# Normalisation parameters and biases of images 1 to 7 computed through device memory and VectorE in a two-layer convolution block

## The chip, the cores and the metric

The kernel runs on one core of a Trainium2 chip. The metric is the device time of one execution in microseconds (us), the median of three runs. The engines are TensorE (PE in the profile; PEld is its weight load), VectorE (DVE), ScalarE (ACT), GpSimd (POOL) and SyncE (SP). Each works through its own list of instructions in order and waits on semaphores for the others. DMAs are issued from SP, ACT or POOL.

## What is computed

Eight images of 384 channels and 64 x 64 positions go through two residual blocks, each with a group normalisation ahead of it (32 groups of 12 channels). Layer 0 is linear attention with rotary positions, layer 1 a gated convolution with an 8 x 8 FFT filter. Cut to what the change touches:

```python
def _gn(v, G=32, eps=1e-5):
    g = v.reshape(B_, G, C_ // G, H_, W_)
    m = jnp.mean(g, axis=(2, 3, 4), keepdims=True)
    s = jnp.var(g, axis=(2, 3, 4), keepdims=True)
    return ((g - m) / jnp.sqrt(s + eps)).reshape(v.shape)

q = apply_rope_2d(conv1x1(x, Wq, bq))
k = apply_rope_2d(conv1x1(x, Wk, bk))
v = conv1x1(x, Wv, bv)
q = jax.nn.elu(to_heads(q) * scale) + 1.0
k = jax.nn.elu(to_heads(k)) + 1.0
kv = jnp.einsum('bhnd,bhne->bhde', k, v)
out = jnp.einsum('bhnd,bhde->bhne', q, kv) / (normalizer + 1e-06)
...
x = x + _L0_conv_ref(_gn(x), ...)
x = x + _L1_conv_ref(_gn(x), ...)
```

## The kernel before

Channels lie on the 128 partitions in three tiles (CT = 3), positions in eight bands of 512. All data are f32. The kernel walks over the images; within one image there are two stages.

*Query stage* (`queries`). For each band, `q_project` (L598) multiplies x with the query weights; DVE adds the bias and turns by the rotary tables (L610, L627), ACT and DVE make elu plus one (L337 to L339); `q_normalise` (L636) and `q_spread` (L660) bring in the normaliser, whose reciprocal DVE writes as `parts` (L652); `project_out` (L677) multiplies with the folded matrix `mt`. At the head of the stage the sums over keys of this image are finished: `kx` is copied by ACT (L566), POOL spreads the key sums into `ks_bd` (L498), DVE puts the heads with the value bias into `kvt_bd` (L571), PE transposes it (`pt`, L583), ACT copies it (`kvt`, L584), PE multiplies (`pm`, L508) and ACT copies `mt` (L515).

*Layer-1 loop.* For each band, layer 1 of this image runs: input projection `pi` (L695), DFT, filter, inverse DFT, the depthwise taps on DVE (L798, `dw`), the gate and the output projection `pw`. Filled in between are the key and value projections (`pk` L438, `pv` L454) and the key sums of the next image. The last band's taps and output run in the next query stage; two of its taps are added by POOL's DMA (`tap`, L781).

Layer 0's normalisation is folded into the weights: the inverse deviation of each channel's group scales the rows of `wk`, `wq` and `wv` (`scale_weight`, L352), and what the mean takes off becomes a bias. The statistics of the next image are streamed during the layer-1 loop (`stream_stats`); what is left is a chain of small steps, `norm_chain`, written as a generator with a `yield` after each step. The query stage of image b pulls it for image b + 1: twice in each of bands 2 to 5, so that its steps lie between the large matmuls. The steps are:

- `mean_and_variance` on DVE (L202 to L207) gives the mean and variance of each channel, `mv`.
- Group mean: three matmuls with a membership matrix (`ps_m`, L273), a copy to `gm` (L291).
- Back to channels: three matmuls (`ps_mc`, L281), difference and square on DVE (L294 to L298).
- Group variance: `ps_v` (L273), `var` (L301), square root on ACT (L303), reciprocal and one Newton step on DVE (L304 to L310).
- Back to channels: `ps_r` (L281), `rs` (L313), and `shift`, minus mean over deviation for each group (L319).

`wk` is then scaled, and `k_bias` (L357, `pbk`) multiplies `shift`, broadcast over 128 columns, with the group sums of the key weights, which `sum_weight` made once with PE (`pg_wk` and others, L345). The result, one row of 384 on all partitions, is added to `bk` (L359). `q_bias` (L365, `pbq`, three matmuls of one column) does the same for the query bias in band 4 of the layer-1 loop, `v_bias` (L375, `pbv`) for the value bias at its end. An f32 matmul counts as two instructions of PE in the profile.

The order of instructions on each engine is not that of the program text: a scheduler places them when the program is built, by priorities and its own estimate of times, and adds all semaphore waits. POOL also issues the DMAs that add layer 1's result to the output in device memory (`out_dram<-y`, L861), and sets the ones columns of the value tiles (`v`, L411). SP issues all other DMAs.

Of the kernel before, what the change touches and what calls it, by code (L numbers as in the profile page):

```python
# [24 lines left out]
NG = 32  # L25
GROUP = C // NG
# [91 lines left out]
def conv_blocks_kernel(ctx: ExitStack, tc: tile.TileContext, a: dict, out: bass.AP, nb: int):  # L118
    nc = tc.nc

    const = ctx.enter_context(tc.tile_pool(name="const", bufs=1))
# [3 lines left out]
    qp = ctx.enter_context(tc.tile_pool(name="qp", bufs=2))  # L125
    small = ctx.enter_context(tc.tile_pool(name="small", bufs=2))
    psum = ctx.enter_context(tc.tile_pool(name="psum", bufs=8, space=bass.MemoryType.PSUM))

    def ps_tile(name):
        return psum.tile([P, 512], F32, tag="ps", name=name)  # L130

    def w_tile(shape, name):
        return work.tile(shape, F32, tag="w", name=name)
# [18 lines left out]
    stats, moments = {}, {}  # L152
# [54 lines left out]
        nc.vector.scalar_tensor_tensor(mv[:, :, 1], s_[:, :, 1], 1.0 / N, s_[:, :, 0], ALU.mult, ALU.subtract)  # L207
        return mv

    group_w = {}  # L210

    for j in range(NBAND - 1):
        load_x(0, j)
# [28 lines left out]
    ident = groups[:, 2 * CT * NG :]  # L242
    of_group = const_tile([NG, C], "of_group", a["of_group"])
    first_wk = load_weight(0, "wk", k_runs)
    load_x(0, NBAND - 1)
    bk_bc = const_tile([P, C], "bk_bc", a["bk"].partition_broadcast(P), nc.sync)
    scale = HD ** -0.5
    halves = (slice(0, 64), slice(64, P))
    w_out = const.tile([P, 2, C], F32, tag="w_out", name="w_out")
# [14 lines left out]
    def norm_chain(b, layer, params):  # L264


        n = f"{layer}_{b}"
        mv = mean_and_variance(b, layer)

        def group_mean(src, name):  # L270
            ps = ps_tile(name)
            for t in range(CT):
                nc.tensor.matmul(  # L273
                    ps[:NG, 0:1], to_group[:, t, :], src[:, t : t + 1], start=(t == 0), stop=(t == CT - 1)
                )
            return ps[:NG, 0:1]

        def to_channels(src, name):
            ps = ps_tile(name)
            for m in range(CT):  # L280
                nc.tensor.matmul(  # L281
                    ps[:, m : m + 1], of_group[:, m * P : (m + 1) * P], src, start=True, stop=True
                )
# [24 lines left out]
        nc.vector.tensor_mul(y, y, var)  # L308
        nc.vector.tensor_scalar(y, y, -0.5, 1.5, ALU.mult, ALU.add)
        nc.vector.tensor_mul(rsg, rsg, y)  # L310
        yield
        rs = small.tile([P, CT], F32, tag=f"rs{layer}", name=f"rs{n}")
        nc.vector.tensor_copy(rs, to_channels(rsg, f"ps_r{n}"))  # L313
        nb_ = small.tile([P, CT], F32, tag=f"nb{layer}", name=f"nb{n}")
        nc.vector.tensor_mul(nb_, minus_mean, rs)  # L315
        params += rs, nb_
        if layer == 0:
            shift = group_tile("shift")
            nc.vector.scalar_tensor_tensor(shift, gm, -1.0, rsg, ALU.mult, ALU.mult)  # L319
            params.append(shift)  # L320

    def normalised(b, j, params, order, name):

        rs, nb_ = params
        h = w_tile([P, CT, BT], f"h{name}_{b}_{j}")
        for t in range(CT):
            dst, src = h[:, t, :], xt[b, j][:, t, :]
            if order is not None:
                blocks, width = order
                dst = dst.rearrange("p (b r c) -> p r b c", b=blocks, r=8, c=width)  # L330
                src = src.rearrange("p (r b c) -> p r b c", b=blocks, r=8, c=width)
            nc.scalar.activation(dst, src, AF.Identity, bias=nb_[:, t : t + 1], scale=rs[:, t : t + 1])  # L332
        return h
# [4 lines left out]
        nc.scalar.activation(e, e, AF.Exp, scale=-1.0)  # L338
        nc.vector.scalar_tensor_tensor(x_, x_, 0.0, e, ALU.max, ALU.add)  # L339

    def sum_weight(w, name):

        p_ = ps_tile(f"pg_{name}")
        for t in range(CT):
            nc.tensor.matmul(p_[:NG, :C], member[:, t, :], w[:, t, :], start=(t == 0), stop=(t == CT - 1))  # L345
        t = const.tile([NG, C], F32, tag=f"group_{name}", name=f"group_{name}")
        nc.scalar.copy(t, p_[:NG, :C])
        group_w[name] = t

    def scale_weight(w, params, factor=1.0):  # L350
        for i in range(CT):
            nc.vector.tensor_scalar(w[:, i, :], w[:, i, :], params[0][:, i : i + 1], factor, ALU.mult, ALU.mult)  # L352

    def k_bias(b, params):

        p_ = ps_tile(f"pbk_{b}")
        nc.tensor.matmul(p_[:, :C], params[2].to_broadcast([NG, P]), group_w["wk"], start=True, stop=True)  # L357
        t = small.tile([P, C], F32, tag="kbias", name=f"kbias_{b}", bufs=1)
        nc.vector.tensor_add(t, p_[:, :C], bk_bc)  # L359
        return t  # L360

    def q_bias(b, params):
        p_ = ps_tile(f"pbq_{b}")
        for m in range(CT):
            nc.tensor.matmul(  # L365
                p_[:, m : m + 1], group_w["wq"][:, m * P : (m + 1) * P], params[2], start=True, stop=True
            )
        t = small.tile([P, CT], F32, tag="qbias", name=f"qbias_{b}")
        nc.vector.scalar_tensor_tensor(t, p_[:, :CT], scale, bqs, ALU.mult, ALU.add)
        return t  # L370

    def v_bias(b, params):

        p_ = ps_tile(f"pbv_{b}")
        nc.tensor.matmul(p_[:, :C], params[2].to_broadcast([NG, P]), group_w["wv"], start=True, stop=True)  # L375
        t = small.tile([P, C], F32, tag="vbias", name=f"vbias_{b}", bufs=1)
        nc.vector.tensor_add(t, p_[:, :C], bv_bc)
        return t

    transposed = {}

# [481 lines left out]
    def layer0_chain(b, prepared):  # L866

        if b >= nb:
            return
        wk = load_weight(b, "wk", k_runs) if b else first_wk  # L870
        params = []
        if b == 0:
            sum_weight(wk, "wk")
        yield from norm_chain(b, 0, params)
        scale_weight(wk, params)
        yield
        prepared += params, wk, k_bias(b, params)

    def chain_of(*chains):
        for c in chains:  # L880
# [8 lines left out]
    class Keys:  # L889


        def __init__(self, b, prepared):
            self.b, self.live = b, b < nb
            if self.live:
                self.params, self.wk, self.bias = prepared
                self.kf = {}

        def project_k(self, j):
# [39 lines left out]
        def prepare(self, j):  # L938

            if self.live and j == 4:  # L940
                self.wq = load_weight(self.b, "wq", QRUNS)
                if self.b == 0:
                    sum_weight(self.wq, "wq")
                scale_weight(self.wq, self.params, scale)
                self.qbias = q_bias(self.b, self.params)
            if self.live and j == NBAND:
                self.wfc = load_weight(self.b, "wfc", k_runs)
                if self.b == 0:
                    self.wv = load_weight(self.b, "wv", k_runs)
                    sum_weight(self.wv, "wv")  # L950
                self.vbias = v_bias(self.b, self.params)

    def queries(b, keys, before_last, late):

# [63 lines left out]
    prepared = []  # L1018
# [1 line left out]
    keys = Keys(0, prepared)  # L1020
    run(keys.project(0))

    bv_bc = const_tile([P, C], "bv_bc", a["bv"].partition_broadcast(P), nc.sync)
    bq = const.tile([P, CT], F32, tag="bq", name="bq")
    for c0, at, n in QRUNS:

        t, p0, quarter, first = at // P, at % P, c0 // QC, c0 % QC
# [15 lines left out]
    for half in halves:  # L1043
        nc.sync.dma_start(w_out[half, 1, :], a["w_out"][P : P + 64, :])

    bqs = const.tile([P, CT], F32, tag="bqs", name="bqs")
    nc.vector.tensor_scalar_mul(bqs, bq, scale)

    filt = const.tile([P, C], F32, tag="filt", name="filt")

# [108 lines left out]
    b = nb - 1  # L1159
# [60 lines left out]
```

## Time and profile before

| | |
|---|---|
| Time, three runs | 3364.33 us median (3363.24 to 3365.47) |
| Span of the profiled execution | 3364.3 us |
| Mean granted TensorE clock | 0.992 |
| Instructions | 53556 |
| HBM read, written | 232.70 MB, 99.88 MB |

A profile shows one execution. Busy time of an engine is the time in which its instructions run; register, branch and semaphore instructions and the issuing of DMAs do not count as busy, apart from what POOL spends on its DMAs' descriptors. The chain of waits goes back from the last instruction to what released each step. In a timeline a row is a run of like instructions: start, duration, engine, line, operation, what it writes and reads, count, and, in brackets, how long the engine stood idle before it and what ended that. PE's matmuls are pipelined, so the duration of a row is longer than its distance to the next one. In the DMA table the last number is the median time from issue to landing.

### The profile page before, as it was taken

To read this page: it belongs to the slowest core of one execution; us is meant where nothing else is said; L and a number is where in the kernel's file an instruction comes from. 1 tells how busy PE (TensorE), PEld (TensorE's weight loads), DVE (VectorE), ACT (ScalarE), POOL (GpSimd) and SP (SyncE) were. 2 spreads that over 40 slices of the span, in tenths; PEclk is the share of its full clock that TensorE was granted. 3 is DMA by queue.
4 is the path that set the end of the run, shared out by engine and by line. 5 is a ranking of instruction groups with operands and counts; after the bars stand their busy time and mean duration, and the time that the engine had idled before them with its cause. 6 is when DMAs were issued, how large, how long until landed. Compare 5 with 4: busy or idle time off the path is not lost.

```text
span 3364.3 us, 53556 instructions
## 1 busy us (share of the span) xinstructions
PE 3300.1 (98%) x21370; PEld 1851.9 (55%) x21370; DVE 2752.5 (82%) x4517; ACT 2034.0 (60%) x4039; POOL 128.8 (4%) x261
## 2 busy tenths in 40 slices
PE   8999999999999999999999999999999999999987
PEld 5544566456654566545665456654566445664454
DVE  6577789967889688896888968888788877989698
ACT  4445666566665566655666656656576565556563
POOL 0000000000000000000000000000000000000000
PEclk9999999999999999999999999999999999999999
DMA  6323335342443423533335343443333431324113
GB/s 217 111 94 100 95 78 128 111 136 67 109 116 110 137 67 94 131 107 120 85 88 126 109 120 76 106 129 107 102 96 94 133 115 54 85 70 121 62 24 53
DMA packets 151502, 343.37 MB, mean 102 GB/s; under 512 B 27365, under 2 KB 38613, under 8 KB 143061
## 3 DMA queue, kind: packets, MB, share of 16 engines
q1 hardware_dynamic: 123844, 282.85, 25.0%
q0 software_dynamic: 27216, 56.89, 11.4%
q8 instruction: 168, 2.75, 0.3%
q14 instruction: 82, 0.66, 0.1%
q10 hardware_dynamic: 192, 0.21, 0.0%
HBM read 232.70 MB, written 99.88 MB: 99 GB/s over the span
## 4 chain that ended last, share of the span: by engine, by line
PE 81%; DVE 11%; ACT 6%; issue 1%; DMA 1%; SPq 0%; DVEq 0%; ACTq 0%
PE pf L677 15%; PE pi L695 14%; PE pk L438 13%; PE pv L454 13%; PE pq L598 9%; DVE dw L798 4%; PE pw L831 4%; PE pb L730 3%; PE pd L709 2%; PE pw L842 2%; PE acc L470 2%; PE acc L483 2%; PE pn L636 1%; ACT qs L338 1%; ACT qs L337 1%
## 5 line engine op out<-in xcount | busy, mean ns | idle before, releaser
L798 DVE SCALAR_TENSOR_TENSOR dw<-ring,w_dw,dw 128x512 f32<-128x512 f32 x1401 | 976.4, 744 | 245.3 <-ACT ring L746 206.2
L438 PE MATMUL pk<-wk,x 128*128 128x384 f32 x1536 | 544.9, 496 | 0.0
L598 PE MATMUL pq<-x,wq 128*128 128x512 f32 x1152 | 527.6, 605 | 2.6 <-ACT mt L515 2.6
L695 PE MATMUL pi<-w_in,hf 128*128 128x384 f32 x1536 | 514.7, 492 | 1.3 <-ACT hf L332 1.3
L677 PE MATMUL pf<-qc,mt 128*128 128x512 f32 x1152 | 512.8, 598 | 0.0
L454 PE MATMUL pv<-wv,x 128*128 128x384 f32 x1344 | 470.0, 488 | 0.0
L438 PEld LDWEIGHTS pk<-wk,x 128*128 128x128 f32 x1536 | 283.5, 191 | 205.3 <-issue 32.5
L695 PEld LDWEIGHTS pi<-w_in,hf 128*128 128x128 f32 x1536 | 288.5, 191 | 196.1 <-issue 4.1
L461 ACT COPY v<-pv 128x384 f32<-128x384 f32 x224 | 108.7, 485 | 424.5 <-PE pv L454 423.3
L454 PEld LDWEIGHTS pv<-wv,x 128*128 128x128 f32 x1344 | 253.6, 190 | 181.4 <-issue 8.4
L677 PEld LDWEIGHTS pf<-qc,mt 128*128 128x128 f32 x1152 | 213.6, 190 | 253.2 <-issue 239.2
L598 PEld LDWEIGHTS pq<-x,wq 128*128 128x128 f32 x1152 | 212.7, 192 | 251.7 <-issue 231.2
L337 ACT ACTIVATE qs<-qc 128x512 f32<-128x512 f32 (+1 forms) x128 | 107.0, 836 | 175.7 <-DVE qc L627 175.7
L681 DVE SCALAR_TENSOR_TENSOR x<-pf,bfc,x 128x512 f32<-128x512 f32 x192 | 137.9, 738 | 91.7 <-PE pf L677 91.6
L179 ACT ACTIVATE differences<-x,shift 128x512 f32<-128x512 f32 x168 | 120.2, 716 | 120.6 <-DVE x L681 120.6
L831 PE MATMUL pw<-gated,w_out 128*128 128x256 f32 x768 | 179.3, 383 | 0.0
L441 DVE TENSOR_TENSOR kc<-pk,kbias 128x384 f32<-128x384 f32 x256 | 140.3, 548 | 40.0 <-PE pk L438 39.9
L702 ACT COPY ht<-pi 128x384 f32<-128x384 f32 x256 | 115.0, 482 | 91.6 <-PE pi L695 88.2
L831 PEld LDWEIGHTS pw<-gated,w_out 128*128 128x128 f32 x768 | 146.7, 192 | 36.9 <-issue 6.5
L337 ACT ACTIVATE ks<-kc 128x1536 f32<-128x1536 f32 x64 | 95.0, 1485 | 99.6 <-DVE kc L445 98.9
L861 POOL DMA_DIRECT2D out_dram<-y x63 | 80.7, 1281 | 1878.0 <-ACT y L856 883.9
L332 ACT ACTIVATE hf<-x,nb,rs 128x512 f32<-128x512 f32 x192 | 146.4, 808 | 2.4 <-DVE nb L315 2.3
(177 smaller groups left out, 4400.0 us busy)
## 6 DMA issues: line engine op xcount, KB each, us to landing
tq<-in_tq SPq DMA_DIRECT2D x64, 1024.0 KB, 4.8
x<-in_x SPq DMA_DIRECT2D x64, 768.0 KB, 6.0
tk<-in_tk SPq DMA_DIRECT2D x64, 768.0 KB, 4.4
out_dram<-x SPq DMA_DIRECT2D x63, 768.0 KB, 3.3
out_dram<-y POOLq DMA_DIRECT2D x63, 768.0 KB, 7.8
xs<-in_x SPq DMA_DIRECT2D x56, 768.0 KB, 5.8
dw<-tap POOLq DMA_DIRECT2D x14, 512.0 KB, 5.1
wk<-in_wk SPq DMA_DIRECT2D x8, 576.0 KB, 3.8
```

The lines of the kernel that those rows point to most:

```text
L179: nc.scalar.activation(out[:, m, :], x_[:, m, :], AF.Identity, bias=shift[:, m : m + 1], accum_out=of_m[0])
L332: nc.scalar.activation(dst, src, AF.Identity, bias=nb_[:, t : t + 1], scale=rs[:, t : t + 1])
L337: nc.scalar.activation(e, x_, AF.Relu, scale=-1.0)
L438: nc.tensor.matmul(pk[:, :C], tokens(t), wks[:, t, :], start=(t == 0), stop=(t == CT - 1))
L441: nc.vector.tensor_add(kc[:, i, :], pk[:, :C], bias)
L454: nc.tensor.matmul(pv[:, :C], xt[b, j][:, t, i * P : (i + 1) * P], wvs[:, t, :], start=(t == 0), stop=(t == CT - 1),)
L598: nc.tensor.matmul(p_, wqs[:, t, m * P : (m + 1) * P], xt[b, j][:, t, :], start=(t == 0), stop=(t == CT - 1),)
L677: nc.tensor.matmul(p_, mt[:, t, m * P : (m + 1) * P], q[:, t, :], start=(t == 0), stop=(t == CT - 1))
L681: nc.vector.scalar_tensor_tensor(xm, p_, bfc[:, m : m + 1], xm, ALU.add, ALU.add)
L695: nc.tensor.matmul(p_[:, :C], h[:, t, i * P : (i + 1) * P], w_in[:, t, :], start=(t == 0), stop=(t == CT - 1),)
L798: nc.vector.scalar_tensor_tensor(acc[:, m], src, wd, acc[:, m], ALU.mult, ALU.add)
L831: nc.tensor.matmul(p_[h][:, m - m0, :], w_out[:, 0, m * P : (m + 1) * P], gated[:, h * HT : (h + 1) * HT], start=(m == m0), stop=False,)
```

## The change

For image 0, the chain stays as it was, except that its bias row is added into a tile that also holds the value bias, and that its `shift` is sent through device memory and read back as a row on all 128 partitions. The group sums of each weight, made once, are now also transposed by PE (`pgt`), so that output channels lie on partitions and 32 groups beside each other (`by_group`).

From image 1 on, `far_chain` takes the place of `norm_chain` for layer 0:

- `mv` is written to a line in device memory by a POOL DMA, and read back with one group of 12 channels on each of 32 partitions.
- DVE makes group mean and variance by sums along the free dimension, ACT takes the root, DVE the reciprocal and the Newton step as before.
- The inverse deviation is written to a second line (12 copies of each), and read back as `rs`, one per channel.
- `shift` is written to a third line, and read back on all partitions.
- `bias_columns` multiplies `by_group` with `shift`, sums over groups, and adds the three biases: all of key, value and query bias at once, as columns.
- `bias_rows` writes key and value bias to a fourth line and reads it back as rows on all partitions. The query bias stays as columns.

The generator has two yields where `norm_chain` has four, so its steps are pulled earlier in the query stage. `q_bias` and `v_bias` are gone; image 0 gets its query and value bias from `bias_columns` at the old places. Layer 1's `norm_chain` is as before. At the start, `bk` and `bv` are also read as columns; `bv` is no longer read as rows.

```diff
+    scratch = ctx.enter_context(tc.tile_pool(name="scratch", bufs=2, space=bass.MemoryType.DRAM))
...
+    def far_chain(b, params):
+        mv = mean_and_variance(b, 0)
+        line = scratch.tile([2 * C], F32, tag="moments", name=f"moments_{b}")
+        nc.gpsimd.dma_start(line.rearrange("(t p i) -> p t i", p=P, i=2), mv)
+        at = small.tile([NG, GROUP, 2], F32, tag="of_groups", name=f"of_groups_{b}", bufs=1)
+        nc.gpsimd.dma_start(at, line.rearrange("(g k i) -> g k i", g=NG, i=2))
+        yield
+        mean, var = at[:, :, 0], at[:, :, 1]
+        one = small.tile([NG, 4], F32, tag="group_steps", name=f"group_steps_{b}", bufs=1)
+        minus, v, rsg, y = (one[:, i : i + 1] for i in range(4))
+        nc.vector.tensor_reduce(minus, mean, mybir.AxisListType.X, ALU.add)
+        nc.vector.tensor_scalar_mul(minus, minus, -1.0 / GROUP)
+        nc.vector.tensor_scalar_add(mean, mean, minus)
+        nc.vector.tensor_mul(mean, mean, mean)
+        nc.vector.tensor_add(mean, mean, var)
+        nc.vector.tensor_reduce(v, mean, mybir.AxisListType.X, ALU.add)
+        nc.vector.tensor_scalar(v, v, 1.0 / GROUP, 1e-5, ALU.mult, ALU.add)
+        nc.scalar.activation(rsg, v, AF.Sqrt)
+        nc.vector.reciprocal(rsg, rsg)
+        nc.vector.tensor_mul(y, rsg, rsg)
+        nc.vector.tensor_mul(y, y, v)
+        nc.vector.tensor_scalar(y, y, -0.5, 1.5, ALU.mult, ALU.add)
+        nc.vector.tensor_mul(rsg, rsg, y)
+        nc.vector.tensor_mul(minus, minus, rsg)
+        nc.vector.tensor_copy(var, rsg.to_broadcast([NG, GROUP]))
+        line = scratch.tile([C], F32, tag="inverse", name=f"inverse_{b}")
+        nc.gpsimd.dma_start(line.rearrange("(g k) -> g k", g=NG), var)
+        rs = small.tile([P, CT], F32, tag="rs0", name=f"rs0_{b}")
+        nc.gpsimd.dma_start(rs, line.rearrange("(t p) -> p t", p=P))
+        params += rs, shift_to_all(b, minus)
+        yield
...
-    def sum_weight(w, name):
+    def sum_weight(w, name, factor=1.0):
...
-        t = const.tile([NG, C], F32, tag=f"group_{name}", name=f"group_{name}")
-        nc.scalar.copy(t, p_[:NG, :C])
-        group_w[name] = t
+        sums = small.tile([NG, C], F32, tag="group_sums", name=f"group_{name}", bufs=1)
+        nc.scalar.copy(sums, p_[:NG, :C])
+        pt = ps_tile(f"pgt_{name}")
+        for m in range(CT):
+            nc.tensor.transpose(pt[:, m * NG : (m + 1) * NG], sums[:, m * P : (m + 1) * P], ident[:NG, :NG])
+        at = places[name] * CT
+        nc.scalar.mul(
+            by_group[:, at : at + CT, :], pt[:, : CT * NG].rearrange("p (m g) -> p m g", m=CT), factor
+        )
+        return sums
...
+    def shift_to_all(b, shift):
+        line = scratch.tile([NG], F32, tag="shift", name=f"shift_line_{b}")
+        nc.gpsimd.dma_start(line.rearrange("(g i) -> g i", i=1), shift)
+        t = small.tile([P, NG], F32, tag="shift_bc", name=f"shift_bc_{b}")
+        nc.gpsimd.dma_start(t, line.partition_broadcast(P))
         return t
...
+    def bias_columns(b, shift_bc, first, last):
+        n = last - first
+        name = f"{b}_{first}"
+        t = small.tile([P, 3 * CT, NG], F32, tag="bias_terms", name=f"bias_terms_{name}", bufs=1)
+        nc.vector.tensor_mul(
+            t[:, :n, :], by_group[:, first:last, :], shift_bc.unsqueeze(1).to_broadcast([P, n, NG])
+        )
+        cols = small.tile([P, 3 * CT], F32, tag="bias", name=f"bias_{name}", bufs=3)
+        nc.vector.tensor_reduce(cols[:, :n], t[:, :n, :], mybir.AxisListType.X, ALU.add)
+        nc.vector.tensor_add(cols[:, :n], cols[:, :n], bias_cols[:, first:last])
+        return cols
+
+    def bias_rows(b, cols, n, to):
+        line = scratch.tile([2 * C], F32, tag="bias_line", name=f"bias_line_{b}")
+        nc.gpsimd.dma_start(line[: n * P].rearrange("(t p) -> p t", p=P), cols[:, :n])
+        nc.gpsimd.dma_start(to, line[: n * P].partition_broadcast(P))
...
         if b == 0:
-            sum_weight(wk, "wk")
-        yield from norm_chain(b, 0, params)
+            sums = sum_weight(wk, "wk")
+            yield from norm_chain(b, 0, params)
+            scale_weight(wk, params)
+            yield
+            first_k_bias(params, sums)
+            prepared += [params[0], shift_to_all(b, params[2])], wk, kv_bias
+            return
+        yield from far_chain(b, params)
         scale_weight(wk, params)
-        yield
-        prepared += params, wk, k_bias(b, params)
+        cols = bias_columns(b, params[1], 0, 3 * CT)
+        rows = small.tile([P, 2, C], F32, tag="kvbias", name=f"kvbias_{b}", bufs=1)
+        bias_rows(b, cols, 2 * CT, rows.rearrange("p i c -> p (i c)"))
+        params.append(cols[:, 2 * CT :])
+        yield
+        prepared += params, wk, rows
...
                 scale_weight(self.wq, self.params, scale)
-                self.qbias = q_bias(self.b, self.params)
+                if self.b == 0:
+                    self.qbias = bias_columns(0, self.params[1], 2 * CT, 3 * CT)
...
-                self.vbias = v_bias(self.b, self.params)
+                    bias_rows(0, bias_columns(0, self.params[1], CT, 2 * CT), CT, self.vbias)
```

More of the change, by code (lines that the diff above doesn't have):

```diff
@@ L208, in mean_and_variance @@
         return mv
-    group_w = {}
+    by_group = const.tile([P, 3 * CT, NG], F32, tag="by_group", name="by_group")
+    bias_cols = const.tile([P, 3 * CT], F32, tag="bias_cols", name="bias_cols")
+    places = {"wk": 0, "wv": 1, "wq": 2}
     for j in range(NBAND - 1):
@@ L245, in conv_blocks_kernel @@
     load_x(0, NBAND - 1)
-    bk_bc = const_tile([P, C], "bk_bc", a["bk"].partition_broadcast(P), nc.sync)
+    kv_bias = small.tile([P, 2, C], F32, tag="kvbias", name="kvbias_0", bufs=1)
+    nc.sync.dma_start(kv_bias[:, 0, :], a["bk"].partition_broadcast(P))
     scale = HD ** -0.5
@@ L352, in scale_weight @@
             nc.vector.tensor_scalar(w[:, i, :], w[:, i, :], params[0][:, i : i + 1], factor, ALU.mult, ALU.mult)
[L354 to L359, printed above, removed]
-        return t
[L362 to L378, printed above, removed]
+    def first_k_bias(params, sums):
+        p_ = ps_tile("pbk_0")
+        nc.tensor.matmul(p_[:, :C], params[2].to_broadcast([NG, P]), sums, start=True, stop=True)
+        nc.vector.tensor_add(kv_bias[:, 0, :], p_[:, :C], kv_bias[:, 0, :])
@@ L894, in __init__ @@
             if self.live:
-                self.params, self.wk, self.bias = prepared
+                self.params, self.wk, self.rows = prepared
+                self.bias, self.vbias = (self.rows[:, i, :] for i in range(2))
+                self.qbias = self.params[2] if self.b else None
                 self.kf = {}
@@ L942, in prepare @@
                 if self.b == 0:
-                    sum_weight(self.wq, "wq")
+                    sum_weight(self.wq, "wq", scale)
                 scale_weight(self.wq, self.params, scale)
-                self.qbias = q_bias(self.b, self.params)
+                if self.b == 0:
+                    self.qbias = bias_columns(0, self.params[1], 2 * CT, 3 * CT)
             if self.live and j == NBAND:
@@ L1021, in conv_blocks_kernel @@
     run(keys.project(0))
-    bv_bc = const_tile([P, C], "bv_bc", a["bv"].partition_broadcast(P), nc.sync)
-    bq = const.tile([P, CT], F32, tag="bq", name="bq")
+    nc.sync.dma_start(bias_cols[:, :CT], a["bk"].rearrange("(t p) -> p t", p=P))
+    nc.sync.dma_start(bias_cols[:, CT : 2 * CT], a["bv"].rearrange("(t p) -> p t", p=P))
+    bq = bias_cols[:, 2 * CT :]
     for c0, at, n in QRUNS:
@@ L1044, in conv_blocks_kernel @@
         nc.sync.dma_start(w_out[half, 1, :], a["w_out"][P : P + 64, :])
-    bqs = const.tile([P, CT], F32, tag="bqs", name="bqs")
-    nc.vector.tensor_scalar_mul(bqs, bq, scale)
+    nc.vector.tensor_scalar_mul(bq, bq, scale)
     filt = const.tile([P, C], F32, tag="filt", name="filt")
```

## The prediction

> **What bounds the kernel now.** I read the page's busy shares first, then the chain of waits.
>
> ```profile
> PE 3300.1 (98%) x21370; PEld 1851.9 (55%) x21370; DVE 2752.5 (82%) x4517; ACT 2034.0 (60%) x4039; POOL 128.8 (4%) x261
> ...
> PE 81%; DVE 11%; ACT 6%; issue 1%; DMA 1%; SPq 0%; DVEq 0%; ACTq 0%
> ```
>
> PE is busy throughout and makes 81% of the chain that ended last, so time taken from PE is time of the kernel wherever PE is not waiting. Next the PE timeline of one image's chain, the one for image 2, which runs inside image 1's query stage (about 571 to 720 us), with its two biases:
>
> ```profile
> 471.90 0.82 PE L365 MATMUL pbq<-shift,group_wq 32*128 32x1 f32 x6
> ...
> 570.02 0.91 PE L375 MATMUL pbv<-group_wv,shift 32*128 32x384 f32 x2
> 570.86 7.99 PE L598 MATMUL pq<-x,wq 128*128 128x512 f32 x18
> ...
> 641.80 0.35 PE L273 MATMUL ps_m<-mv,groups 128*32 128x1 f32 x6
> ...
> 651.21 0.60 PE L281 MATMUL ps_mc<-gm,of_group 32*128 32x1 f32 x4
> ...
> 660.08 0.35 PE L273 MATMUL ps_v<-d,groups 128*32 128x1 f32 x6
> ...
> 669.37 0.60 PE L281 MATMUL ps_r<-rsg,of_group 32*128 32x1 f32 x4
> ...
> 678.23 0.91 PE L357 MATMUL pbk<-group_wk,shift 32*128 32x384 f32 x2
> ```
>
> These small matmuls stand between large ones with no idle time; what each takes is the distance to the next row's start. Last, where PE does wait for another engine in that stage (waits of PE; columns: us in total, times, longest):
>
> ```profile
> PE pt L583 <- DVE kvt_bd L571: 10.7, 21, 1.1
> ...
> PE prb L660 <- DVE parts L652: 6.0, 7, 0.9
> ```
>
> So at the head of each query stage (584 to 620 us here) DVE sets the pace: `pt` waits for `kvt_bd`, `prb` for `parts`, 0.85 us at 618.47. From 625 on DVE is ahead: `parts` of band 2 is written at 630.5 and its `prb` starts at 633.60.
>
> **What is removed.** From the timeline, per image: `ps_m` 0.28 (641.80 to 642.08); `ps_mc` 0.67 (651.21 to 652.16, less 0.28, what twelve `prb` take alone); `ps_v` 0.28; `ps_r` 0.66 (669.37 to 670.31, less 0.28); `pbk` 0.84. Together 2.73 us, in a part of the stage where PE is not waiting; seven chains, 19.1 us. `pbq` takes 0.76 in the layer-1 loop, where PE is busy 229.8 of 230 us: seven times, 5.3 us. `pbv` takes 0.84, but lies just ahead of the DVE-paced head; there only DVE's saving counts, the `vbias` addition (573.91 to 574.38), 0.47 us, seven times 3.3 us. Image 0 loses its `pbq` and `pbv` (1.6 us) and gets three transposes for each; no row here is a 32-row transpose, so between nothing and the 0.75 that six matmuls of that size take in `pbq`: I take 0.4 each, a gain of 0.8. The third set of transposes falls into the start, where PE waits 2.06 us for `mv` anyway: nothing, and 0.4 if it didn't. Sum: 28.5 us.
>
> **What is added, and where it waits.** The chain moves from bands 2 to 5 of the query stage to its head. In the built program's lists DVE has the group sums straight after the six `kvt_bd` and before the turn of query band 1; ACT has the square root, with its table load, between `kx` and `kvt`; a further exponential table load stands before the exponential of band 1. POOL has `moments` and `of_groups` ahead of the last `y` store and the twelve `ks_bd` copies. Today's rows on DVE and ACT:
>
> ```profile
> 585.74 0.15 DVE L207 SCALAR_TENSOR_TENSOR mv<-mvs 128x3 f32<-128x3 f32 x1
> ...
> 590.27 1.79 DVE L571 SCALAR_TENSOR_TENSOR kvt_bd<-vbias,kx 64x64 f32<-64x64 f32 x6
> 592.10 0.75 DVE L610 SCALAR_TENSOR_TENSOR qc<-pq,qbias,tq 128x512 f32<-128x512 f32 x1
> ...
> 605.38 0.35 DVE L652 SCALAR_TENSOR_TENSOR parts<-part,take_off,rn 128x128 bf16<-128x128 bf16 x1 [0.40 <-ACT part L651]
> ```
> ```profile
> 592.54 0.48 ACT L584 COPY kvt<-pt 128x384 f32<-128x384 f32 x1 [2.30 <-PE pt L583]
> ```
>
> Everything here comes 0.47 earlier without `vbias`: `mv` is complete at 585.4, DVE gets to the group sums at 591.6. If the data is there, seven dependent small operations follow; in image 0's chain such operations start 0.19 apart (26.22, 26.42, 26.61), so 1.33; root and reciprocal take 0.45 more (0.20 on ACT, hand-overs as at 27.41 to 27.98). The turn of band 1 starts at 593.5, not 591.6. ACT, held at the root, copies `kvt` at 593.2 to 593.7; PE needs that at 594.4, so `pm` does not wait. But ACT's queue behind it is late: two `qs` 1.4, two `tap` 1.3, six `mt` 2.9, then relu, one more `mt`, the new table load of 1.28 (the row of every table load), exponentials. I get the last exponential of band 1 to 604.9, DVE's end of band 1 to 606.1, and `parts` to 607.75 where it is now at 605.73; through the next band, whose ACT order also differs a little, to 1.9 us late at band 1's `prb`. So PE loses 1.9 net of the 0.47 counted above, 2.4 gross. Gross it could be 1.2, if the table load is hidden, or 3.0, if the remaining small operations also hold band 2. Six images (stages 1 to 6): 14.4 us. DVE's work outside the head is about even: chain and `kbias` out, two 128x288 operations in, and it is 3 us ahead there.
>
> In image 0's stage nothing of this costs: DVE idles 7.1 us before 160.48 and 6.2 us before 181.62; `rs` and the shifted bias hold it for some 3 us around 169, and POOL's `ks_bd`, then behind the bias line, ends some 2 us late at 179.3 where `pn` comes at 187.3. Without that cover, 3 us.
>
> The rest of the DMAs, `shift`, `inverse`, `rs`, the bias line and its broadcast, have from 601 to 644 (`wk` scaling) and from 655 to about 725 (first `pk`); behind them on POOL wait `v` memsets, first used after 740. They cost nothing; if the broadcast (384 KB) came after 725, its lateness would fall on PE. On SP only the first image's bias loads change, amid 6 us of loading.
>
> **The unknown: the round trip.** Call S the time that DVE waits at the group sums for `moments` out and `of_groups` in. Nearest rows (DMA issues; last columns KB each, us to landing):
>
> ```profile
> out_dram<-y POOLq DMA_DIRECT2D x63, 768.0 KB, 7.8
> ...
> dw<-tap POOLq DMA_DIRECT2D x14, 512.0 KB, 5.1
> ...
> wq<-in_wq SPq DMA_DIRECT2D x16, 48.0 KB, 3.2
> ```
>
> POOL is busy 1.28 us to issue `y` (384 pieces, as `moments` has), and the first packet starts 1.86 us after the issue in the packet records; 0.90 and 1.47 for the 128 pieces of `tap`. Upper bound: the pair lands like `y` and `tap`, 12.9 us, 598.3, S = 6.7. Lower bound: no wait, S = 0, since DVE arrives 6.2 us after `mv`. `moments` is nearest to the 48 KB `wq`, also 384 tiny pieces, 3.2 us, plus the later first packet of a POOL issue: 3.7. `of_groups` has 32 pieces of 96 bytes: 1.5 to the first packet and about 1 for the rest (a 32 KB load, `sq`, lands in 1.8 in all). 585.5 + 3.7 + 2.5 = 591.7; engines are 75% busy from 585 to 606, so I take S = 0.3. Each us of S costs PE a us in six stages: 1.8 us.
>
> [...]
>
> **Sum.** The profiled span is 3364.3 us and the median of the runs 3364.33, so nothing lies around it. 3364.3 - 28.5 + 14.4 + 1.8 = 3352.0.
>
> **Rivals.**
> *Slower: the round trip.* DVE and, through the root, ACT stand still until `of_groups` lands; behind them wait `kvt`, `pm`, `mt`, band 1 and PE. Price 6 us per us of S; even at S = 2.35, over 0.2% slower from 3.5. At S = 5: 3364.3 - 28.5 + 14.4 + 30 = 3380. For it: POOL's landings above, and that both DMAs share engines with `x` and `tq` loads. Against: they carry 3 KB each.
> *Cancelled.* S between 1.2 and 3.5: about 3364. The same would come of a gross loss of 4.7 us a stage.
> *Hidden.* ACT and DVE make up the delay: 3364.3 - 28.5 = 3336. Against it: `prb` already waits for `parts` there.
> That the matmuls are not removed is excluded: PE's list after is the old one without them, in the same order.
>
> **How the numbers follow.** A measurement of this kernel can tell about 0.2% (6.7 us) from no change. Forecast (3344 to 3357.5): 0.47. Hidden: 0.07. Cancelled: 0.18. Slower: 0.28. So faster 0.54, same 0.18, slower 0.28. The forecast's own range is its row: gross loss 1.2 to 2.4 with S up to 1.2. The range for the time, 3344 to 3381, leaves out most of "hidden" and the slower case beyond S = 5.
>
> **What would show it.** PE busy should fall by some 30 us. In stages 1 to 6, `prb` should wait for `parts` about 1.9 us longer in all; `of_groups` should land 6 to 7 us after `mv` is complete; DVE's wait for that DMA is S. The landing is what makes me wrong first: at 9 us the gain is gone. A second: `pm` waiting for `kvt` with S small, so ACT's order weighs more than I gave it.

## The result, and the profile after

The change made the kernel slower: 3377.06 us median (3375.13 to 3378.78) against 3364.01 us for the kernel before, run beside it. The ratio is 1.0037, with a 95% interval of 1.0025 to 1.0048. The profiled execution of the changed kernel has a span of 3373.3 us, 9.0 more than the 3364.3 before. The medians are 13.1 us apart: times lie 1.8 us above their spans, so the execution profiled before was some 2 us slower than its median, and the one profiled after is the fastest of its four.

First the busy time of TensorE and the shares of the chain of waits, from the page of the changed kernel.

```profile
PE 3276.2 (97%) x21133; PEld 1832.2 (54%) x21133; DVE 2761.4 (82%) x4521; ACT 2021.8 (60%) x4036; POOL 168.0 (5%) x321
...
PE 79%; DVE 7%; issue 5%; ACT 5%; DMA 2%; POOL 1%; SPq 0%; DVEq 0%; POOLq 0%; ACTq 0%
```

TensorE is busy for 23.9 us less than before (3300.1), so the matmuls are gone as intended, and yet the end comes later. What is lost must be TensorE's waiting. These are its waits, and below them those of VectorE that end with one of the new DMAs (us in total, times, longest).

```profile
PE prb L709 <- DVE parts L701: 22.8, 13, 3.0
...
PE pt L632 <- DVE kvt_bd L620: 13.6, 21, 1.5
PE pr L579 <- ACT kx L575: 9.4, 1, 9.4
...
PE pm L557 <- ACT kvt L633: 4.1, 4, 1.7
...
DVE group_steps L338 <- DMA of_groups<-moments: 21.3, 7, 6.8
...
DVE wk L397 <- DMA rs<-inverse: 13.4, 1, 13.4
```

`prb` waited 6.0 us before, 7 times, at most 0.9; now 22.8, up to 3.0 a time. `pr` is new: one wait of 9.4 us in image 0's stage. So is `pm`, which stood for `kvt` in four stages. VectorE stands for `of_groups` in all seven chains, and once, for 13.4 us, for `rs`.

The timeline of image 1's query stage shows the head of such a stage (start, duration, what it is, idle time before it and what ended that).

```profile
591.16 0.80 POOL L331 DMA_DIRECT2D moments<-mv  x1 [5.09 <-DVE mv L208]
597.12 0.54 POOL L333 DMA_DIRECT2D of_groups<-moments  x1 [5.17 <-DMA moments<-mv]
...
595.25 1.79 DVE L620 SCALAR_TENSOR_TENSOR kvt_bd<-kvbias,kx 64x64 f32<-64x64 f32 x6
599.54 0.15 DVE L338 TENSOR_REDUCE group_steps<-of_groups 32x1 f32<-32x12 f32 x1 [2.51 <-DMA of_groups<-moments]
...
600.92 0.20 ACT L345 ACTIVATE group_steps<-group_steps 32x1 f32<-32x1 f32 x1 [4.40 <-DVE group_steps L344]
601.03 0.45 ACT L633 COPY kvt<-pt 128x384 f32<-128x384 f32 x1
...
615.49 0.35 PE L709 MATMUL prb<-parts,expand 32*128 32x128 bf16 x12 [3.04 <-DVE parts L701]
```

`moments` is issued at 591.16 and has landed when POOL issues `of_groups`, 5.96 us later; that takes another 2.4. VectorE was through with `kvt_bd` at 597.04 and stands 2.51 us. ScalarE stands behind it at the root, 4.40 us, with `kvt` next in its list. TensorE pays at `prb` of band 0, and in some stages at `pm`. Over the stages of images 1 to 6 this wait of VectorE is (21.3 - 6.8) / 6 = 2.4 us each.

In image 0's stage POOL's and VectorE's timelines read so.

```profile
162.42 0.77 POOL L429 DMA_DIRECT2D bias_line<-bias  x1 [3.06 <-DVE group_steps L350]
163.18 0.65 POOL L354 DMA_DIRECT2D inverse<-of_groups  x1
...
172.40 0.57 POOL L430 DMA_DIRECT2D kvbias<-bias_line  x1 [8.05 <-DMA bias_line<-bias]
172.95 0.78 POOL L356 DMA_DIRECT2D rs<-inverse  x1
...
180.33 0.75 DVE L397 TENSOR_SCALAR wk<-wk,rs 128x384 f32<-128x384 f32 x2 [13.45 <-DMA rs<-inverse]
```

The scaling of `wk` for image 1 has been placed ahead of the rest of band 1's turn, and waits for `rs`. That is read from a line (`inverse`) whose write was issued at 163.18, behind image 0's bias line. POOL stood 8.05 us for the bias line, but `inverse` itself took 9.1 us to land, until 172.3, so the place in the queue held the read of `rs` by only some 0.7 us.

A third thing shows only in the granted clock. The window view gives, for a stretch, the busy time of each engine (number of instructions in brackets), the TensorE clock, DMA share and GB/s. First two stretches of the kernel before, in image 4's stage: the wait at `pt`, and what follows.

```profile
1816.00:1819.00 3.00, 1.38 (x5) 0.38 (x4) 2.83 (x8) 1.01 (x4) 1.78 (x4) 1.00 0.19 41
1819.60:1822.60 3.00, 3.00 (x5) 1.35 (x4) 2.03 (x4) 2.90 (x5) 1.27 (x7) 0.50 1.06 165
```

And three of the changed kernel, in image 2's stage: the wait at `pt`, what follows, and what follows the wait at `prb`.

```profile
1004.00:1006.00 2.00, 0.67 (x3) 0.29 (x4) 1.80 (x7) 1.40 (x2) 0.00 (x0) 1.00 0.00 0
1007.00:1010.00 3.00, 3.00 (x5) 1.01 (x3) 1.03 (x7) 0.00 (x0) 2.63 (x9) 0.50 0.52 50
...
1025.00:1028.00 3.00, 3.00 (x16) 1.28 (x5) 3.00 (x6) 0.00 (x0) 0.00 (x0) 0.50 0.24 5
```

Here, after TensorE has waited for a us or two, its clock is halved for some 3.4 us, and 1.7 us are lost on top of the wait. Before, this came in two of the stages of images 1 to 6; afterwards in each of them, and in image 2's for three such stretches.

So the span can be taken apart. "Stage" is the time from the first `pq` of an image to the start of its last `pf`; "idle" is the stage less TensorE's busy time, and "clock" is the sum over windows of one us of what is missing from full clock. The rest is TensorE's work. Seven loops lie between the stages.

| us | before | after |
|---|---|---|
| loops, each | 254.8 to 255.0 | 253.2 to 253.6 |
| stage of image 0 | 155.7 | 162.9 |
| stages of images 1 to 6, sum | 927.6 | 940.6 |
| of these, idle | 15.7 | 38.3 |
| clock | 3.4 | 13.7 |
| the rest | 908.5 | 888.6 |

Loops -10.9, image 0's stage +7.2, the other six -19.9 of work, +22.6 idle and +10.2 clock, and -0.2 elsewhere: the 9.0 of the spans.

### The profile page after: what moved, and what is told of

It reads as the page before. It is cut to its first block, busy times and chain, and to the rows that moved or that the text cites. A ratio compares the mean times of both kernels' runs of the same rounds, so it can differ in the third digit from the quotient of the medians.

```text
span 3373.3 us, 53209 instructions
## 1 busy us (share of the span) xinstructions
PE 3276.2 (97%) x21133; PEld 1832.2 (54%) x21133; DVE 2761.4 (82%) x4521; ACT 2021.8 (60%) x4036; POOL 168.0 (5%) x321
## 4 chain that ended last, share of the span: by engine, by line
PE 79%; DVE 7%; issue 5%; ACT 5%; DMA 2%; POOL 1%; SPq 0%; DVEq 0%; POOLq 0%; ACTq 0%
PE pf L726 15%; PE pi L744 14%; PE pk L487 13%; PE pv L503 12%; PE pq L647 8%; PE pw L880 4%; PE pb L779 3%; PE pd L758 2%; DVE dw L847 2%; PE pw L891 2%; PE acc L519 2%; PE acc L532 1%; PE pn L685 1%; ACT mt L564 1%; ACT qs L668 1%
## 5 line engine op out<-in xcount | busy, mean ns | idle before, releaser
L503 PEld LDWEIGHTS pv<-wv,x 128*128 128x128 f32 x1344 | 253.6, 190 | 181.4 <-issue 8.4
L726 PEld LDWEIGHTS pf<-qc,mt 128*128 128x128 f32 x1152 | 213.6, 190 | 253.2 <-issue 236.6
L490 DVE TENSOR_TENSOR kc<-pk,kvbias 128x384 f32<-128x384 f32 x256 | 140.8, 550 | 39.0 <-PE pk L487 38.8
L377 DVE SCALAR_TENSOR_TENSOR qc<-qc,qs 128x512 f32<-128x512 f32 (+1 forms) x128 | 122.2, 955 | 34.3 <-ACT qs L376 33.5
```

The source lines that it names most:

```text
L490: nc.vector.tensor_add(kc[:, i, :], pk[:, :C], bias)
L503: nc.tensor.matmul(pv[:, :C], xt[b, j][:, t, i * P : (i + 1) * P], wvs[:, t, :], start=(t == 0), stop=(t == CT - 1),)
L726: nc.tensor.matmul(p_, mt[:, t, m * P : (m + 1) * P], q[:, t, :], start=(t == 0), stop=(t == CT - 1))
```

## The experiments

### Hold the scaling of wk in image 0's stage

```diff
+        rs = small.tile([P, CT], F32, tag="rs_late", name=f"rs_late_{b}")
+        nc.vector.scalar_tensor_tensor(rs, held[b - 1][:, :CT], 0.0, params[0], ALU.mult, ALU.add)
-        scale_weight(wk, params)
+        scale_weight(wk, [rs])
...
+            if j == 2:
+                held[b] = normaliser[3]
```

> The changed kernel with one more small VectorE operation per image that ties the scaling of wk to parts of band 3, so that VectorE no longer waits for rs at the head of image 0's query stage; the rest of the order stays. Theory A (image 0's stage lost its 7.2 us because VectorE stood 13.45 us for rs ahead of band 1's turn): that stage, from its first pq to its last pf, falls from 162.9 to 153 to 155 us, the other stages stay at 155.5 to 158.7, the time is about 3368. Rival B (the group sums and root at 159 to 162 us held VectorE and ScalarE there): the stage stays above 160, the time at 3375 to 3377.

3382.12 us, ratio 1.0054 (1.0039 to 1.0069): not faster but slower. Image 0's stage went to 166.8. VectorE's timeline says why:

```profile
182.99 0.46 DVE L420 TENSOR_TENSOR bias_terms<-by_group,shift_bc 128x288 f32<-128x288 f32 x1 [14.42 <-DMA shift_bc<-shift_line]
```

`wk` no longer stood there, but the sums for the bias columns did, and they wait for `shift_bc`, which is behind `rs` in POOL's queue. A wait took the place of the one removed. Neither theory had named it; that the group sums alone hold this stage (B) is not shown by it either.

### Take the round trip's wait away, leave the rest

```diff
+    lines = [a["groups"].rearrange("p i -> (p i)")[: 2 * C]]
...
         nc.gpsimd.dma_start(line.rearrange("(t p i) -> p t i", p=P, i=2), mv)
+        line, lines[0] = lines[0], line
...
+        nc.vector.tensor_scalar(minus, kvt_bd[:NG, 0, 0:1], 0.0, 0.0, ALU.mult, ALU.add)
         nc.vector.tensor_reduce(minus, mean, mybir.AxisListType.X, ALU.add)
```

> The kernel of the run before (wk's scaling held to band 3), and of_groups is read from the line of the image before, which lies in device memory long ahead (other values, so another normalisation); moments is still written; one small VectorE operation keeps the group sums behind kvt_bd, where they are now. So VectorE no longer waits for the round trip; its order and ScalarE's in stages 1 to 6 are unchanged. Theory A (a us of that wait, S, costs a us of each of these stages): S of about 2.4 falls to 0, each of stages 1 to 6 is 2.2 to 2.5 us shorter than in the run before (157.0 to about 154.6), the time is 13 to 15 us below the run before, about 3354. Rival C (ScalarE's order, the root and the further table load ahead of kvt and mt, sets the loss): these stages shorten by less than 1 us, the time by less than 6.

This kernel leaves out the right statistics: `of_groups` has those of the image before. It is a test of time alone.

3349.57 us, ratio 0.9960 (0.9948 to 0.9973), 32.6 below the run before. 9.2 of that is image 0's stage (166.8 to 157.6), which the small operation also changed: image 1's chain moved behind `kvt_bd` there, so that stage is no clean test. The stages of images 1 to 6 went from 944.4 to 920.8 in all, 3.9 each, where VectorE's wait S for the round trip had been 2.75 us each in the run before. Idle time fell by 14.1 us, the clock's loss from 13.7 to 5.1. So S weighs most, and theory C falls; but the gain is more than theory A's 2.2 to 2.5 us a stage: a us of S cost 23.6 / 16.5 = 1.43 us, not one. What is left is the chain itself at the head, in the timeline of TensorE:

```profile
607.65 0.34 PE L715 MATMUL prb<-parts,expand 32*128 32x128 bf16 x12 [2.55 <-DVE parts L707]
```

### Image 0's value bias by TensorE

```diff
+    nc.sync.dma_start(kv_bias[:, 1, :], a["bv"].partition_broadcast(P))
...
-                    sum_weight(self.wv, "wv")
-                    bias_rows(0, bias_columns(0, self.params[1], CT, 2 * CT), CT, self.vbias)
+                    sums = sum_weight(self.wv, "wv")
+                    p_ = ps_tile("pbv_0")
+                    nc.tensor.matmul(p_[:, :C], self.params[2].to_broadcast([NG, P]), sums, start=True, stop=True)
+                    nc.vector.tensor_add(self.vbias, p_[:, :C], self.vbias)
```

> The changed kernel, but image 0's value bias is made as before, by a matmul with the group sums, so that POOL's queue in image 0's stage holds no bias line and no read of it. Rival D (the read of rs stood behind the read of the bias line on POOL, which waited 8 us): rs comes 8 us earlier, image 0's stage falls from 162.9 to about 155, the time to about 3369. Theory A (the line inverse itself takes 8.9 us to land, issued at 163.2, so rs can be read at 172.1 at the earliest instead of 172.95): VectorE's wait for rs shortens by 1 to 2 us, the stage is 161 to 163, the time 3375 to 3377.

3369.23 us, ratio 1.0014 (1.0005 to 1.0024), 7.8 less than the changed kernel. Image 0's stage is 158.7; POOL's and VectorE's timelines in it:

```profile
162.14 0.61 POOL L355 DMA_DIRECT2D inverse<-of_groups  x1
...
169.87 0.77 POOL L357 DMA_DIRECT2D rs<-inverse  x1 [4.05 <-DMA inverse<-of_groups]
...
173.52 0.75 DVE L398 TENSOR_SCALAR wk<-wk,rs 128x384 f32<-128x384 f32 x2 [6.61 <-DMA rs<-inverse]
```

Neither theory has it right. VectorE's wait is halved, 6.8 us less, but not by the queue. `inverse` is issued 1.0 us earlier and lands 7.5 us after its issue instead of 9.1; the read of `rs` then stands 0.3 us in the queue instead of 0.7, and lands after 3.6 us instead of 7.4. So the queue (rival D) made 1.4 us, and 5.4 came from the two lines landing sooner when the bias line and its broadcast are not in flight beside them. The other half of the wait is the round trip of `inverse` and `rs` itself. That the time came out at rival D's 3369 is luck: the stage is at 158.7, not 155. The two profiled spans are 6.9 us apart, of which 4.2 are this stage and 1.7 the stretch after the last stage, whose length varies between the runs.

### Move the chain behind the round trip to bands 3 to 5

```diff
+        nc.vector.tensor_scalar(minus, held[b - 1][:NG, 0:1], 0.0, 0.0, ALU.mult, ALU.add)
         nc.vector.tensor_reduce(minus, mean, mybir.AxisListType.X, ALU.add)
```

(`held` is filled as in the first run; the small operation reads `parts` of band 3.)

> The changed kernel with one more small VectorE operation per image that ties the group sums to parts of band 3, so that the whole chain behind the round trip runs in bands 3 to 5 of the query stage, where norm_chain's steps were; the round trip itself is issued where it was. Theory A (the loss is all at the head: S, the seven operations, the root and its table load, and rs in image 0's stage; TensorE's saving is real): stage 0 about 153, stages 1 to 6 about 151.5 to 152.5 each, prb of band 0 back at 35 us from the stage's start, the time 3335 to 3342. Rival E (the chain costs as much wherever VectorE and ScalarE take it, since they pace the later bands as well): stages 1 to 6 stay at 155 or more, the time 3355 to 3370.

3371.67 us, ratio 1.0023 (1.0012 to 1.0033). `prb` of band 0 no longer waited, and up to the `prb` of band 1 the stages of images 1 to 6 had 2.8 to 3.7 us of idle time (2.6 before the change, 5.7 to 7.4 with it); but these stages came to 946.2, 5.6 longer than in the changed kernel. In the waits of VectorE:

```profile
DVE wk L400 <- DMA rs<-inverse: 51.6, 7, 7.9
```

The scaling of `wk` was let go at band 3 with the sums, so VectorE now stood there for the second round trip, 7.4 us a time. That is a fault of my cure: it held one reader of a line and not the next. Whether rival E holds this run can't say; the next one can.

### Hold both

```diff
+        for _ in range(3):
+            yield
+        rs, shift_bc = small.tile([P, CT], F32, tag="rs_late", name=f"rs_late_{b}"), params[1]
+        nc.vector.scalar_tensor_tensor(rs, held[b - 1][:, :CT], 0.0, params[0], ALU.mult, ALU.add)
+        scale_weight(wk, [rs])
+        nc.vector.scalar_tensor_tensor(shift_bc, held[b - 1][:, :NG], 0.0, shift_bc, ALU.mult, ALU.add)
+        cols = bias_columns(b, shift_bc, 0, 3 * CT)
...
+            if j in (2, 4):
+                held[b] = normaliser[j + 1]
```

> As the run late (group sums tied to parts of band 3), and the scaling of wk and the bias sums are tied to parts of band 5 as well, since in the run late VectorE stood up to 7.9 us at wk for rs, after it was released at band 3. Nothing then stands in VectorE's list ahead of its data. Theory A (all of the loss is VectorE waiting for the lines in device memory, and what follows from TensorE waiting): TensorE's idle time in each of stages 0 to 6 is 2.6 to 3.5 us, as in the kernel before, stages 1 to 6 last about 151 to 152.5, the time is 3331 to 3342. Rival E (the added VectorE and ScalarE work itself costs as much as the matmuls did): idle time of 5 us or more in these stages, the time 3350 or more.

3339.62 us, ratio 0.9924 (0.9909 to 0.9939): theory A, inside its range. Every DMA of the change is still there, and the lines take as long to write (`moments` 5.5, `inverse` 9.5, `bias_line` 10.7 us in the median). Two things differ from the changed kernel: nothing in VectorE's list stands ahead of its data, and the chain's small operations, the root and its table load have left the head. This run doesn't part the two; the run without the round trip's wait, above, gives 3.9 us a stage to the first.

```profile
PE pt L635 <- DVE kvt_bd L623: 13.7, 21, 1.5
...
PE prb L712 <- DVE parts L704: 5.3, 7, 0.9
```

TensorE's waits at `prb` are those of the kernel before, and the one at `pr` is gone; no wait of VectorE for one of the new lines is left. Image 0's stage is 152.8, the stages of images 1 to 6 915.5 in all, with 20.6 idle and 6.8 of clock. Four of these six, those with a stretch of half clock, lasted 152.9 to 153.4 us, a little over theory A's 152.5.

### One more matmul where TensorE waits

```diff
         pt = ps_tile(f"pt_{b}")
+        for _ in range(1):
+            nc.tensor.matmul(pt, ident, xt[b, 1][:, 0, :], start=True, stop=True)
```

In the kernel before, and in the version of the run above.

> The kernel before with the one further matmul of 128 by 128 by 512 ahead of pt in images 1 to 7, in the bank that pt overwrites; the order on all other engines is the same. In the kernel before, the granted clock is halved for 3.4 us after the wait at pt in stages 4 and 6, and in no other of stages 1 to 6, which cost these two 1.7 us each. Theory F (the wait sets it off): no halved clock in stages 1 to 6, these stages 153.9 to 154.3 throughout, the time 3360 to 3362. Rival G (another cause): still some 1.7 us in two of the stages, or in others, the time 3364 or more.

3360.81 us, ratio 0.9989 (0.9980 to 0.9999). The stages of images 0 to 6 are now 154.0 us each, and no stretch of half clock is left in them in this profile, which is of the fastest of the ten executions (granted clock 0.995; the others 0.993 to 0.995, against 0.992 to 0.993 before). Image 0's got no such matmul, so what spared it is something else (see the last section). The stretch of image 4's stage that followed the wait at `pt`, in the window view:

```profile
1816.00:1819.00 3.00, 3.00 (x10) 1.43 (x8) 2.21 (x4) 2.95 (x6) 1.17 (x5) 1.00 1.08 183
```

> As the run late_both, and one further matmul of 128 by 128 by 512 is put ahead of pt in images 1 to 7; it writes pt's own bank, which pt then overwrites, so nothing changes in what is computed. It stands where TensorE waits for kvt_bd (1.06 us before). Theory F (a wait of a us or two at the head halves TensorE's granted clock for 3.4 us in some images, 1.7 us a time): fewer or no such stretches in stages 1 to 6, and a time 0 to 5 us below that of late_both. Rival G (the halved clock has another cause than the waits): as many such stretches as in late_both, and the time the same or up to 3 us longer.

3335.89 us, ratio 0.9910 (0.9896 to 0.9925), the fastest of all. One stretch of half clock is left in the stages of images 1 to 6, instead of four; it follows a wait of 1.89 us at `pn`, which the added matmul doesn't fill. Theory F holds in both kernels: the waits set the half clock off. These counts are from one profile of each; the 3.7 us that either kernel gained are from all its runs.

### The round trip from SyncE's queue

```diff
-        nc.gpsimd.dma_start(line.rearrange("(t p i) -> p t i", p=P, i=2), mv)
+        nc.sync.dma_start(line.rearrange("(t p i) -> p t i", p=P, i=2), mv)
...
-        nc.gpsimd.dma_start(at, line.rearrange("(g k i) -> g k i", g=NG, i=2))
+        nc.sync.dma_start(at, line.rearrange("(g k i) -> g k i", g=NG, i=2))
```

> The changed kernel with moments and of_groups issued from SyncE's queue, not POOL's; the order of VectorE, ScalarE and TensorE in stages 1 to 6 is the same. Theory H (POOL's queue makes the round trip slow: a later first packet, and issues one behind the other): moments lands in 3 to 4 us, VectorE's wait for of_groups falls from 2.4 to below 1 us, each of stages 1 to 6 is 1.5 us or more shorter, the time 3360 to 3368. Rival I (the 384 small pieces and the loads that fill the DMA engines there make it slow, whichever queue issues them): moments still takes 5 us or more, the wait stays at 2 us or more, the time at 3372 or more.

3383.16 us, ratio 1.0051 (1.0036 to 1.0066). SyncE's queue and VectorE in image 1's stage:

```profile
594.20 0.38 SPq L331 DMA_DIRECT2D moments<-mv  x1
594.68 1.18 SPq L145 DMA_DIRECT2D x<-in_x  x1
599.26 0.33 SPq L333 DMA_DIRECT2D of_groups<-moments  x1
...
604.21 0.15 DVE L338 TENSOR_REDUCE group_steps<-of_groups 32x1 f32<-32x12 f32 x1 [3.87 <-DMA of_groups<-moments]
```

`moments` has landed 5.06 us after its issue here (median 4.9, against 5.5 from POOL), so POOL's queue makes at most some 0.6 us of it. `of_groups` is worse, 4.1 in the median against 2.4: it follows a 768 KB load of `x`. Rival I holds for the wait and the time. Of its two causes, the profile of the changed kernel tells the weight: in image 0's stage the same write, from the same queue, finds the DMA engines idle.

```profile
153.16 0.77 POOL L331 DMA_DIRECT2D moments<-mv  x1 [2.92 <-DVE mv L208]
157.09 0.52 POOL L333 DMA_DIRECT2D of_groups<-moments  x1 [3.15 <-DMA moments<-mv]
```
```profile
153.16:156.81 3.65, 3.65 (x13) 1.74 (x12) 0.00 (x0) 0.00 (x0) 0.77 (x1) 1.00 0.04 1
591.16:596.83 5.67, 3.88 (x10) 1.42 (x8) 5.13 (x11) 5.34 (x9) 0.80 (x1) 1.00 0.63 243
```

There `moments` landed in 3.6 us at a DMA share of 0.04; in image 1's stage it took 5.7 at 0.63, and 5.1 to 5.9 in the stages of images 1 to 6. From SyncE's queue it still took 4.9 in the median, 1.3 more than these 3.6, so most of the difference is neither POOL nor what VectorE does beside it. Some 2 us go with the loads beside the write; the small pieces and the trip itself take the 3.6.

## Why the prediction was wrong, step by step

*What is removed (28.5 us): right.* The loops lost 1.6 us each, all of `pbq` and `pbv` (0.76 + 0.84). TensorE's work in the stages of images 1 to 6 fell by 19.9 us by difference, 3.3 each, where 2.73 was counted; the rest isn't explained. That `pbv` would come back in part as waiting is also seen: the wait at `pt` grew from 1.06 to 1.50 us.

*The chain at the head (14.4 us): right in size.* It was to bring 2.4 us a stage, and 0.37 more idle time from `pbv` (0.84 of TensorE's work goes, 0.47 of VectorE's): 2.8. With S taken away, stages 1 to 3 had 2.6 us more idle time than before. Stages 4 to 6 had 1.4 more, next to a stretch of half clock each.

*S = 0.3: wrong, the first failure.* It was 2.4 us. The step that failed is the landing of `moments`, put at 3.7 us after the 48 KB load of `wq`; it took 5.5 in the median, and 5.96 from its issue to that of `of_groups` in image 1's stage. `of_groups` at 2.5 was right (2.4). The 3.7 is what the write took in image 0's stage (3.6), where the DMA engines are idle. I had noted that they are 75% busy at the other heads, and gave that 0.2 us (591.7 against 591.6 makes 0.1, taken as 0.3); it cost about 2.

*"Each us of S costs PE a us": wrong, the second failure.* The price was 1.43, since longer waits of TensorE also halved its clock: 10.2 us more in six stages than before, a term that the sum doesn't have. The rows were in the profile of the kernel before, where two of the six stages are 1.7 us longer than their neighbours for no other reason; I didn't compare the stages.

*"In image 0's stage nothing of this costs": wrong, the third.* It cost 162.9 - 152.8 = 10.1 us against the version in which nothing stands. The cover I named, VectorE's idle time, was real, but idle time before an instruction doesn't cover a wait that is placed in the middle of the turn; and I gave `rs` and the shifted bias some 3 us, where there `inverse` needed 9.1 us to land and `rs` 7.4 more.

The landings, from the DMA table of the changed kernel (KB each, median us from issue to landing):

```profile
moments<-mv POOLq DMA_DIRECT2D x7, 3.0 KB, 5.5
of_groups<-moments POOLq DMA_DIRECT2D x7, 3.0 KB, 2.4
...
inverse<-of_groups POOLq DMA_DIRECT2D x7, 1.5 KB, 8.9
...
rs<-inverse POOLq DMA_DIRECT2D x7, 1.5 KB, 6.1
...
bias_line<-bias POOLq DMA_DIRECT2D x1, 1.5 KB, 9.7
```

*The rivals.* The slower one, the round trip, named the mechanism and the place, but not the price: it asked for S over 3.5. With S = 2.4 the prediction's own sum gives about 3364.6, no change, which is the rival "cancelled"; the clock and image 0's stage made it slower. VectorE's work did not lengthen POOL's issue of `moments`: that took 0.80 us at 591.16, while VectorE was at work on the taps (590.83 to 592.44), and 0.77 at 153.16, while VectorE was idle (0.00 us busy up to 156.81).

*The rest of the DMAs: right.* `shift`, `inverse`, `rs` and the bias line of images 2 to 7 cost nothing that shows: neither TensorE nor VectorE waits for them in the changed kernel.

*The start of the sum.* That nothing lies around the span was read from two different executions; every listed time is 1.8 us above its span.

## What to carry to other kernels

Here work moved off the bounding engine through device memory was worth what it freed only when nothing that engine waits for stood behind the reader of the line (3339.62 us, against 3377.06); check every reader, since holding one hands the wait to the next (from `wk` to `bias_terms` in one run, from `group_steps` to `wk` in another). The scheduler placed the readers of small DMAs in the busiest stretch here; three tiny operations an image that read a late result put them where there is slack, and turned +0.37% into -0.76%. Price a wait of TensorE with the clock that it costs, not with its length alone: a us of S came to 1.43 us here.

## What was not expected of the hardware

Three gaps of 1.06, 0.28 and 0.28 us between small matmuls halved TensorE's clock for 3.4 us in two of six stages of the kernel before, and the same gaps left it alone in the four others, with the same instructions around them. Which of them are struck can be read from the profile: all its stretches of half clock start a whole multiple of 3.413 us apart (those in the stages at 204.87, 1819.37 and 2638.57, so 473 and then 240 of them). Cut into windows on that grid, images 3 and 4 read so (window, TensorE's busy time first, the clock third from the end):

```profile
1406.36:1409.77 3.41, 1.97 (x6) 0.52 (x4) 2.98 (x8) 1.72 (x5) 1.53 (x3) 1.00 0.31 120
1409.77:1413.19 3.42, 3.23 (x9) 1.67 (x10) 2.44 (x5) 2.75 (x5) 2.00 (x11) 1.00 1.01 126
...
1815.96:1819.37 3.41, 1.79 (x6) 0.64 (x5) 3.24 (x8) 1.11 (x5) 2.08 (x5) 1.00 0.30 47
1819.37:1822.78 3.41, 3.41 (x5) 1.35 (x4) 2.26 (x4) 3.13 (x5) 1.45 (x8) 0.50 1.03 159
```

In images 4 and 6 all three gaps fall into one window, in which TensorE is busy for 1.79 us, and the next window has half the clock. In images 1, 2, 3 and 5 an edge of the grid parts the gaps, the window is busy for 1.97 us or more, and nothing follows. No single border holds for all kernels, though: in the changed kernel a window with 1.59 us busy (from 610.86) was spared. In image 0's stage one gap of 2.57 us lies in one window, and half clock follows; in the run with the added matmul TensorE stood as long there (busy for 0.53, 0.00, 0.00 and 0.90 us in the four windows of one us from 198.87), and nothing followed. No stretch in these stages shows where that execution's grid lay, so that an edge parted this gap is an estimate. One matmul, which brought the first of the three gaps from 1.06 to 0.21 us (image 4's), kept the clock in the stages of images 1 to 6 of the one profile taken.

A line of 1.5 KB that the kernel lays out in pieces of 4 bytes took 8.9 us to land (`inverse`), and 3.0 KB so laid out 10.3 us (`bias_line`), more than the 7.8 us of a 768 KB store of `y` in the kernel before; 0.1 KB (`shift_line`) took 5.2. For `inverse` the loads beside it are not the reason: in image 0's stage it took 9.1 us at a DMA share of 0.03.
